# Ten shared parts between the experts instead of eight, and the slots' tokens made in two steps

## The chip, the core and the metric

The kernel runs on one core of one Trainium2 chip. The metric is the device time of one execution, in microseconds (us), as the median of several runs. The profile is one execution recorded by the hardware profiler; its span is the time from the first to the last instruction that the profiler saw. The engines go by the profile's short names: PE is TensorE (PEld its weight loads), DVE is VectorE, ACT is ScalarE, POOL is GpSimd, and SP is the engine that issues most DMAs. [...]

## The reference

One transformer block on x of shape (4, 512, 512), all in float32:

```
x = x + cross_attention(layernorm(x), context)          # 16 heads of 32; 257 image and 1344 text keys
x = x + moe(layernorm(x))                               # 2048 tokens, width D = 512

moe(h):
    scores = sigmoid(h @ router_w.T)                    # E = 32 experts, in 8 groups of 4
    keep the 3 groups whose two best (scores + bias) sum highest, then the 4 best experts in them
    w = chosen scores / their sum * 2.5
    for each expert e, the first C = 80 of its tokens (in order of token number) fill its slots
    Y[e] = (silu(Xp[e] @ W_gate[e]) * (Xp[e] @ W_up[e])) @ W_down[e]     # inner width I = 256
    out[token] += w * Y[e]                              # scattered back by token
    shared = (silu(h @ shared_gate.T) * (h @ shared_up.T)) @ shared_down.T     # inner width 512
    return out + shared
```

The shared expert sees every token; a routed expert sees only the 80 rows gathered for it.

## The kernel before

**Attention.** The four batches are worked on one after another: queries, keys and values, scores, exponentials, weighted values. The output projection, the second layernorm and the router's logits of batch b (`residual`) are interleaved with the attention of batch b + 1. For the last batch they have no attention to hide in and go into the stage described next. The normalised tokens are written to `xw_d` in device memory (one row for each token, with its 32 routing weights behind it) and, transposed, to `xnT_d`.

**The shared expert as parts.** `shared()` cuts the shared expert into parts of equal size: each is 8 matmul instructions in the profile. For every batch n of 512 tokens there are four `gate` parts (ending in a SiLU on ScalarE, L944), four `up` parts (ending in a product on VectorE, L949, which reads the gate) and four `down` parts. The downs of batches 0 and 1 end in an addition on VectorE (L967) to a tile fetched by SP (L955), which SP then stores (L968). Those of batches 2 and 3 end in a copy on ScalarE and an accumulating DMA (L972). The function gives three lists: 32 parts that run before the experts, 8 (gates and ups of batch 3) to go between the experts, and 8 (downs of batches 2 and 3) for the end. In the first list, parts 0 to 7 are gates and ups of batch 0; 8 to 19 are those of batch 1 with the downs of batch 0 among them; 20 to 31 are those of batch 2 with the downs of batch 1 among them, in the order gate, up, down, down, gate, up, down, down, gate, up, gate, up. `fetch_x` (L932) loads the next batch's transposed tokens, 1 MB, when the third gate of a batch is issued; the third gate of batch 2 is part 28.

**The stage before the experts.** A loop over the first list (index i) issues a part and then what is hung on it. The `residual` steps of the last batch hang on parts 8 to 15: fetch of the input tile (L449 adds a bias on GpSimd), projection and addition (L455), normalisation (L220), transpose (L468) and logits (L476). Every fourth part issues the three weight loads of one expert (L908), up to expert 5. `deal(i)` hands out the routing.

**The routing.** `routing(b, space)` is a list of 73 small items for 512 tokens: a sigmoid on ScalarE, then some 50 short VectorE operations that choose groups and experts (the last choice is the third L585), the store of the routing weights (L597, issued by SP), an iota on GpSimd (L610), `ranks` (four transposes on TensorE, L606, of the chosen experts, and an operation that forms a sort key, L607), and a search of 19 items that finds the 80 lowest token numbers of each expert: ten times the 8 largest (L619), and nine times these struck out (L621). Batches 0 and 1 are routed during the attention. Batch 2's list, `first`, starts behind part 2; batch 3's, `second`, at part 16, when the last logits are there. `deal(i)` hands out items in order until an amount `spent` reaches `(i - 1) * SHARE`; an item adds 0.8 when fewer than 20 are left in its list, otherwise 0.3. Items are issued behind part i on each engine, and `spent` runs on from the first list to the second.

**The tokens.** `tokens()` is called ahead of part 30. On VectorE it turns the 32 x 80 table `best` into token numbers `past` (L917 and L918), transposes it on TensorE (L920), and casts the result to integers, `tok` (L921). Behind it six indirect gathers (L993) are issued on GpSimd's queue, one for each of experts 0 to 5.

**The expert loop.** For expert e: gate and up (64 instructions, `gate_up`, L225 with SiLU at L1017 and product at L1018), weight loads for expert e + 6, the transposes of expert e + 2's tokens (`turn`, L1004, copied by L1006), the down projection of expert e - 1 (L1023), its scaling on ScalarE (L1027), its indirect scatter that adds to the output (L1028, on GpSimd's queue), and the gather for expert e + 5 behind it (L993). The parts of the second list are spread by `done * (E - 4) < n_between * e`. The third list follows the loop.

Of the kernel before, what the change touches and what calls it, by code (L numbers as in the profile page):

```python
# [58 lines left out]
@with_exitstack  # L59
def xattn_moe_kernel(ctx: ExitStack, tc: tile.TileContext, a: dict, out: bass.AP):  # L60
    nc = tc.nc

    dram = ctx.enter_context(tc.tile_pool(name="dram", bufs=1, space=DRAM))
    x1_d = dram.tile([T, D], F32, name="x1_d")

    xw_d = dram.tile([T, D + E], F32, name="xw_d")
    xnT_d = dram.tile([P, NC, T], F32, name="xnT_d")
    den_d = dram.tile([B * NC, 2 * NG4, L], F32, name="den_d")
    rec_d = dram.tile([B * NC, 2 * NG4, L], F32, name="rec_d")

    const = ctx.enter_context(tc.tile_pool(name="const", bufs=1))
    ident = const.tile([P, P], F32, name="ident")
    make_identity(nc, ident)
    mhalf = const.tile([P, 8], F32, name="mhalf")
    nc.gpsimd.memset(mhalf, -0.5)
    logits = const.tile([P, NT, E], F32, name="logits")

    with tc.manual_schedule():
        body(tc, a, ident, mhalf, logits, x1_d, xw_d, xnT_d, den_d, rec_d, out)
# [30 lines left out]
def body(ctx, tc, a, ident, mhalf, logits, x1_d, xw_d, xnT_d, den_d, rec_d, out):  # L110
# [14 lines left out]
    def psum(dt=F32):  # L125

        shape = [P, 512] if dt is F32 else [P, NQ, P]
        banks.append(banks.pop(0))
        return ring.tile(shape, dt, name="ps", tag=f"bank{banks[-1]}")
# [8 lines left out]
    def wide(name, keep=False):  # L138

        n = wides.pop(0)  # L140
        t = pt.tile([P, NC, 512], F32, name=name, tag=f"wide{n}")
        if keep:
            return t, n
        wides.append(n)
        return t

    def rowt(name):
        return row.tile([P, D], F32, name=name, tag="row")

    def held(name):  # L150
        return hold.tile([P, D], F32, name=name, tag="hold")
# [9 lines left out]
    def weight(name, tile_=None, tag=None):  # L161
        t = w.tile([P, NC, D], F32, name=name, tag=tag or name) if tile_ is None else tile_
        nc.sync.dma_start(t, a[name])
        return t
# [57 lines left out]
    def project(ps, lhsT, rhs):  # L222

        for c in range(NC):
            nc.tensor.matmul(ps, lhsT=lhsT(c), rhs=rhs(c), start=c == 0, stop=c == NC - 1)  # L225
# [678 lines left out]
    def expert_weights(e, *names):  # L904

        for name in names or ("W_gate", "W_up", "W_down"):
            t = wgp.tile([P, NI, D] if name == "W_down" else [P, NC, I], F32, name=name, tag=name)
            nc.sync.dma_start(t, a[name][e])  # L908
            weights.setdefault(e, []).append(t)

    SHARE = 2.4
    AHEAD, WEIGHTS = 6, 6

    def tokens():

        past = ew.tile([E, CAP], F32, name="past", bufs=1)
        nc.vector.tensor_scalar(past, best, T + 0.5, float(T), ALU.is_gt, ALU.mult)  # L917
        nc.vector.scalar_tensor_tensor(past, past, float(T), best, ALU.add, ALU.subtract)  # L918
        ps = psum()
        nc.tensor.transpose(ps[:CAP, :E], past, ident[:E, :E])  # L920
        nc.vector.tensor_copy(tok, ps[:CAP, :E])  # L921

    def shared():


        units = [[], [], []]
        downs = []
        xTs = {0: first_xT[0]}

        def fetch_x(n):  # L930
            xTs[n] = wide("xT")
            nc.sync.dma_start(xTs[n], xnT_d[:, :, n * L:(n + 1) * L])  # L932

        for n in range(B):
            t = {}

            def gate(ic, n=n, t=t):
                if ic == 0:
                    t["hT"] = wide("hT")
                if ic == 2 and n + 1 < B:  # L940
                    fetch_x(n + 1)
                ps = psum()
                project(ps, lambda k: sg[:, k, ic * P:(ic + 1) * P], lambda k: xTs[n][:, k, :])
                nc.scalar.activation(t["hT"][:, ic, :], ps, AF.Silu)  # L944

            def up(ic, n=n, t=t):
                ps = psum()
                project(ps, lambda k: su[:, k, ic * P:(ic + 1) * P], lambda k: xTs[n][:, k, :])
                nc.vector.tensor_tensor(t["hT"][:, ic, :], t["hT"][:, ic, :], ps, ALU.mult)  # L949
                if n == 0 and ic == NC - 1:  # L950
                    wides.append(first_xT[1])

            def fetch(j, n=n, t=t):
                t[j] = held("x1r")
                nc.sync.dma_start(t[j], x1_d[n * L + j * P:n * L + (j + 1) * P, :])  # L955

            def down(j, n=n, t=t, fetch=fetch):
                rows = slice(n * L + j * P, n * L + (j + 1) * P)
                if n < BEFORE:
                    if j == 0:  # L960
                        fetch(0)
                    if j + 1 < NQ:
                        fetch(j + 1)
                ps = psum()
                project(ps, lambda k: t["hT"][:, k, j * P:(j + 1) * P], lambda k: sd[:, k, :])
                if n < BEFORE:
                    nc.vector.tensor_tensor(t[j], t[j], ps, ALU.add)  # L967
                    nc.sync.dma_start(out[rows, :], t[j])  # L968
                    return
                y = rowt("ys")  # L970
                nc.scalar.copy(y, ps)
                nc.gpsimd.dma_start(out[rows, :], y, accum_op=ALU.add)  # L972

            to = units[n == B - 1]
            if n == B - 1:
                units[0] += downs
                downs = []
            for ic in range(NC):
                to += [partial(gate, ic), partial(up, ic)]
                if ic < 2:  # L980
                    to += downs[2 * ic:2 * ic + 2]
            downs = [partial(down, j) for j in range(NQ)]
            if n >= BEFORE:
                units[2] += downs
                downs = []
        return units
# [51 lines left out]
        return weights, gather, turn, gate_up, down  # L1038

    units, between, ends = shared()  # L1040
    wo = weight("o_w", wide("wo"))
    for u in units[:2]:
        u()
# [19 lines left out]
    def deal(i):  # L1063

        nonlocal spent
        while spent < (i - 1) * SHARE and (first or second):
            todo = first or second
            spent += 0.8 if len(todo) < 2 * CAP // 8 else 0.3
            todo.pop(0)()

    for i, u in enumerate(units):
        if i < 2:
            continue
        if i == len(units) - 2:
            for f in first + second:
                f()
            first, second = [], []
            tokens()
            for e in range(AHEAD):
                gather(e)  # L1080
        if i == ready:

            space = mid.tile([P, 2, L], F32, name="rb")
            second = sum(routing(B - 1, space.rearrange("p k t -> p (k t)")), [])
            deal(i)
        u()
        for f in side.get(i, ()):
            f()
        later.step()
        deal(i)  # L1090
        if i % 4 == 0 and i // 4 - 1 < WEIGHTS:
            expert_weights(i // 4 - 1)
# [57 lines left out]
```

## Time and profile before

| | us |
|---|---|
| median of three runs | 1709.5 |
| lowest and highest | 1707.76, 1710.98 |
| the profiled execution, its own time | 1712.07 |
| its span | 1710.4 |
| last matmul groups of the attention, about | 1338 |
| parts 2 to 31 of the shared expert, with the last residual and two routings | 1340 to 1464 |
| expert loop | 1466 to 1674 |
| downs of batches 2 and 3, and the last stores | 1674 to 1710 |

The first four rows are measured times and the profile's span; the others are read off the timeline of TensorE. In lines of the timeline the first two numbers are the start and the length in us, then engine, line, operation, the tile written and read, and in brackets how long the engine was idle before it and who released it. In the list of waits the numbers are the total, the number of waits and the longest. In the table of stages each pair is an engine's busy time with its instruction count, in the order PE, PEld, DVE, ACT, POOL, then the granted clock of TensorE (1.00 is full), the mean busy share of the 16 DMA engines and GB/s.

### The profile page before, as it was taken

How to read it: one execution, taken by the hardware profiler on the slowest of the kernel's cores; microseconds unless marked ns; L12 is line 12 of the kernel's file. 1: busy time of each engine (PE TensorE's matmuls, PEld its weight loads, DVE VectorE, ACT ScalarE, POOL GpSimd, SP SyncE). 2: the span in 40 equal slices, each digit the busy share in tenths (PEclk: the TensorE clock that was granted, in tenths of full speed). 3: DMA queues.
4: the chain of work that ended last, by engine and by line, in shares of the span. 5: the costliest groups of instructions: out<-in, count | busy, mean ns of one | idle time of the engine just before them, and what ended most of it. 6: DMA issues, size and time to landing. Idle time of an engine off the chain costs nothing. (4 is left out here: it accounts for less than half of the span.)

```text
span 1710.4 us, 29446 instructions
## 1 busy us (share of the span) xinstructions
PE 1682.0 (98%) x11753; PEld 881.9 (52%) x11753; DVE 980.2 (57%) x2012; ACT 653.4 (38%) x1382; POOL 870.3 (51%) x622
## 2 busy tenths in 40 slices
PE   8999999999999999999999999999999999999997
PEld 4564444446544444565444445654443454677673
DVE  4765554857555557876666579766656777111110
ACT  2135456611454565114555651145557310111111
POOL 3246977333669753336688533376884110333332
PEclk9999999999999999999999999999999999999999
DMA  7000000312000004020001040200002365699864
GB/s 232 1 1 1 27 27 2 114 65 71 29 2 26 26 3 164 15 81 20 2 26 27 14 153 21 83 36 10 5 15 89 114 217 188 209 285 287 268 168 61
DMA packets 67817, 136.30 MB, mean 80 GB/s; under 512 B 16096, under 2 KB 28512, under 8 KB 65632
## 3 DMA queue, kind: packets, MB, share of 16 engines
q1 hardware_dynamic: 60400, 119.91, 20.9%
q0 software_dynamic: 6272, 12.92, 4.1%
q8 instruction: 93, 1.52, 0.4%
q10 hardware_dynamic: 1008, 1.59, 0.3%
q14 instruction: 44, 0.36, 0.1%
HBM read 111.58 MB, written 22.81 MB: 79 GB/s over the span
## 5 line engine op out<-in xcount | busy, mean ns | idle before, releaser
L372 ACT ACTIVATE pT<-ps 128x512 f32<-128x512 f32 (+1 forms) x832 | 429.7, 603 | 342.2 <-PE ps L371 334.1
L334 DVE TENSOR_REDUCE mx<-ps 128x1 f32<-128x512 f32 (+1 forms) x576 | 330.9, 616 | 265.0 <-PE ps L320 265.0
L387 POOL TENSOR_TENSOR acc<-acc,pT 128x1024 f32<-128x1024 f32 x192 | 445.6, 2357 | 3.0 <-ACT pT L372 2.6
L379 PE MATMUL po<-pT,v 128*32 128x512 f32 (+2 forms) x1792 | 222.0, 603 | 0.0
L290 PEld LDWEIGHTS ps<-v_w,cT 128*128 128x128 f32 (+1 forms) x1408 | 168.9, 186 | 102.2 <-DVE mx L334 56.1
L371 PE MATMUL ps<-qT,kT 32*128 32x512 f32 (+1 forms) x1664 | 213.7, 587 | 0.0
L320 PE MATMUL ps<-kT,qT 32*128 32x512 f32 (+1 forms) x1536 | 206.2, 549 | 0.0
L290 PE MATMUL ps<-v_w,cT 128*128 128x128 f32 (+1 forms) x1408 | 197.7, 284 | 0.0
L231 PE MATMUL ps<-cT,wk 128*128 128x512 f32 (+1 forms) x384 | 156.8, 554 | 5.9 <-DMA wk<-in_k_w 5.9
L308 DVE TENSOR_REDUCE mx<-ps 128x1 f32<-128x512 f32 (+2 forms) x256 | 128.0, 561 | 5.8 <-PE ps L305 5.8
L1028 POOL DMA_INDIRECT out<-y,tok x32 | 45.5, 1420 | 136.8 <-DMA out<-y,tok 68.4
L231 PEld LDWEIGHTS ps<-cT,wk 128*128 128x128 f32 x384 | 71.1, 194 | 75.9 <-issue 55.7
L368 PEld LDWEIGHTS <-pick 32*128 32x128 bf16 (+1 forms) x832 | 21.6, 91 | 165.8 <-issue 164.0
L298 ACT COPY v<-ps 128x128 f32<-128x128 f32 (+1 forms) x208 | 59.7, 287 | 117.7 <-PE ps L290 117.3
L238 POOL TENSOR_TENSOR sq_k<-sq_k,sq 128x512 f32<-128x512 f32 (+2 forms) x48 | 49.6, 1033 | 103.3 <-ACT sq L235 103.0
L1018 DVE TENSOR_TENSOR ehT<-ehT,ps 128x160 f32<-128x160 f32 x32 | 10.3, 321 | 159.7 <-ACT ehT L1017 159.7
L394 POOL TENSOR_TENSOR acc<-pT 128x1024 f32<-128x1024 f32 x24 | 56.1, 2359 | 86.9 <-ACT pT L372 54.3
L387 POOL TENSOR_TENSOR pT<-pT 65x1024 f32<-65x1024 f32 x24 | 56.0, 2354 | 86.7 <-PE po L379 77.9
L387 DVE TENSOR_TENSOR acc<-acc,pT 128x1024 f32<-128x1024 f32 (+1 forms) x72 | 97.7, 1404 | 2.1 <-ACT pT L372 2.1
L320 PEld LDWEIGHTS ps<-kT,qT 32*128 32x128 f32 x1536 | 82.0, 183 | 30.8 <-issue 10.1
L379 PEld LDWEIGHTS po<-pT,v 128*32 128x32 f32 (+2 forms) x1792 | 34.7, 107 | 118.6 <-issue 109.3
L368 PE MATMUL ps<-mT,pick 32*128 32x512 bf16 (+1 forms) x832 | 82.5, 385 | 2.5 <-ACT mT L359 2.5
(209 smaller groups left out, 2194.4 us busy)
## 6 DMA issues: line engine op xcount, KB each, us to landing
W_gate<-in_W_gate SPq DMA_DIRECT2D x32, 512.0 KB, 4.9
W_up<-in_W_up SPq DMA_DIRECT2D x32, 512.0 KB, 5.2
W_down<-in_W_down SPq DMA_DIRECT2D x32, 512.0 KB, 5.7
rb<-rec_d SPq DMA_DIRECT2D x64, 128.0 KB, 2.7
xt<-in_x SPq DMA_DIRECT2D x30, 256.0 KB, 2.7
cT<-in_ctxT SPq DMA_DIRECT2D x7, 1024.0 KB, 9.3
wki<-in_k_img_w SPq DMA_DIRECT2D x4, 1024.0 KB, 10.4
wo<-in_o_w SPq DMA_DIRECT2D x4, 1024.0 KB, 5.0
```

The costliest lines, as they stand in the source:

```text
L231: nc.tensor.matmul(ps[:, :n], lhsT=wt[:, k, c * P:(c + 1) * P], rhs=xT[:, k, to], start=k == 0, stop=k == NC - 1)
L290: nc.tensor.matmul(ps[lo:hi, :], lhsT=cTs[bl][:, k, at:at + hi - lo], rhs=ws[bl == NB - 1][:, k, c * P:(c + 1) * P], start=k == 0, stop=k ...
L298: nc.scalar.copy(v[:n, t, :], ps[:n])
L308: nc.vector.tensor_reduce(mx[:, qt, g, bl:bl + 1], ps[:, :n], AX.X, ALU.max, negate=True)
L320: nc.tensor.matmul(ps[:, j * n:(j + 1) * n], lhsT=qT[r:r + HD, c, q * P:(q + 1) * P], rhs=kT[r:r + HD, c, k0:k0 + n], start=True, stop=True,)
L334: nc.vector.tensor_reduce(mx[:, qt, g, i:i + 1], ps[:, :m], AX.X, ALU.max, negate=True)
L368: nc.tensor.matmul(ps[:n], lhsT=pick[r:r + HD, kind(t), :n], rhs=mT[r:r + HD, :], start=True, stop=False)
L371: nc.tensor.matmul(ps[:n], lhsT=kT[r:r + HD, c, t * P:t * P + n], rhs=qT[r:r + HD, c, :], start=False, stop=True)
L372: nc.scalar.activation(pT[:n, g, :], ps[:n], AF.Exp)
L379: nc.tensor.matmul(po[r:r + HD, :], lhsT=v[rows, t, r:r + HD], rhs=pT[rows, g, :], start=start, stop=stop)
L387: (nc.vector if idle else nc.gpsimd).tensor_tensor(to[rows, h, :], to[rows, h, :], pT[rows, h, :], ALU.add)
L394: (nc.vector if idle else nc.gpsimd).tensor_tensor(acc[:, h, :], pTs[0][:, h, :], pTs[1][:, h, :], ALU.add)
```

## The change

Two parts, the last gate and the last up of batch 2, go from the end of the first list to the front of the second. The first list is then 30 parts long and ten parts are spread between the experts. `tokens` is split. Its two VectorE operations, now `kept_tokens`, are issued ahead of part 27 (they were ahead of part 30), and what is left of `tokens`, with the six gathers, ahead of part 28, which again is two parts before the list ends. What is left of the routing by then is issued ahead of part 27. `SHARE`, by which `deal` hands out the routing, rises from 2.4 to 2.7.

```diff
-    SHARE = 2.4
+    SHARE = 2.7
     AHEAD, WEIGHTS = 6, 6
 
-    def tokens():
+    def kept_tokens():
 
         past = ew.tile([E, CAP], F32, name="past", bufs=1)
         nc.vector.tensor_scalar(past, best, T + 0.5, float(T), ALU.is_gt, ALU.mult)
         nc.vector.scalar_tensor_tensor(past, past, float(T), best, ALU.add, ALU.subtract)
+        return past
+
+    def tokens(past):
+
         ps = psum()
         nc.tensor.transpose(ps[:CAP, :E], past, ident[:E, :E])
         nc.vector.tensor_copy(tok, ps[:CAP, :E])
...
     units, between, ends = shared()
+    units, between = units[:-2], units[-2:] + between
     wo = weight("o_w", wide("wo"))
...
     for i, u in enumerate(units):
         if i < 2:
             continue
-        if i == len(units) - 2:
+        if i == len(units) - 3:
             for f in first + second:
                 f()
             first, second = [], []
-            tokens()
+            past = kept_tokens()
+        if i == len(units) - 2:
+            tokens(past)
             for e in range(AHEAD):
                 gather(e)
```

## The prediction

> **What bounds the kernel now.** I read the page first, then the table of stages, the waits of TensorE alone, and the chain and the timelines around each of those waits.
>
> ```profile
> PE 1682.0 (98%) x11753; PEld 881.9 (52%) x11753; DVE 980.2 (57%) x2012; ACT 653.4 (38%) x1382; POOL 870.3 (51%) x622
> 1440.00:1480.00 40.00, 38.09 (x158) 21.65 (x156) 14.47 (x30) 3.08 (x6) 8.21 (x8) 1.00 0.53 166
> 1560.00:1600.00 40.00, 39.45 (x251) 29.23 (x249) 4.70 (x12) 6.29 (x13) 12.59 (x11) 1.00 0.92 285
> 1600.00:1640.00 40.00, 37.19 (x227) 26.65 (x228) 4.61 (x13) 6.46 (x13) 14.41 (x13) 1.00 0.94 281
> ```
>
> TensorE (first pair of numbers of a stage row, then weight loads, VectorE, ScalarE, GpSimd, clock, DMA share, GB/s) has work almost all the time. No matmul is added or dropped, so only its idle time can change. From the last attention to the end it idles in three stages: 1.9 us in 1440 to 1480, 0.55 in 1560 to 1600, 2.8 in 1600 to 1640. Its waits from 1330 us on name them:
>
> ```profile
> PE ps L1004 <- DMA xp<-xw_d,tok: 2.3, 1, 2.3
> PE ps L920 <- DVE past L918: 1.2, 1, 1.2
> PE ps L1004 <- ACT ehT L1017: 0.9, 2, 0.5
> PE ps L225 <- DVE xpT L1006: 0.7, 1, 0.7
> ```
>
> **The loop's stall.** The chain shows where the first of them comes from:
>
> ```profile
> 1584.46 7.10 DMA out<-y,tok
> 1592.38 5.94 DMA out<-y,tok
> 1599.14 6.34 DMA out<-y,tok
> 1608.03 6.11 DMA xp<-xw_d,tok
> 1614.27 0.47 PE ps L1004 x4
> ```
>
> Each expert's scatter (L1028) waits for the landing of the one before, and the gather of expert e+6 (L993) is issued behind the scatter of e on the same queue. From the scatter of expert 4 (1505.64 us) to that of expert 18 (1606.30) there are 14 periods in 100.66 us: 7.19 each. TensorE needs 5.53 us for an expert (1478.88 to 1484.41) and 3.43 for a shared part. With eight parts over 28 turns that is 5.53 + 8/28 x 3.43 = 6.51: quicker than the chain of DMAs, so its lead of gathers is used up. The timeline has the turns (L1004) at 1565.19, 1600.37, 1606.20 and 1614.27 later than the matmuls ahead of them allow by 0.61, 0.64, 0.28 and 2.50 us: **4.03 us**. The first two are booked to ScalarE, but gathers 17 and 22 were issued at 1558.45 and 1594.11, 6.7 and 6.3 us earlier, about a landing (6.11 in the chain). I read all four as gathers.
>
> **What moving two parts into the loop does.** Two matmul groups of 8 (2 x 3.43 us) leave from before the loop. The count in the source puts the ten parts after experts 1, 3, 6, 9, 12, 15, 17, 20, 23, 26, where eight stood after 1, 4, 8, 11, 15, 18, 22, 25. At the turns made beside experts 15 and 20, TensorE has done one part more than before (3.43 us), beside 21 and 22 two more (6.86). Up to there the missed time added up to 0.61, 1.25, 1.53 and 4.03. The cover suffices at each, by 2.83 us at the last. The chain itself starts alike: two parts lie ahead of the output of expert 4 before and after. I take **-4.0 us**; kept between 0 and -4.0.
>
> **Tokens a part sooner.** Before, L917 and L918 stand on VectorE behind the product of the last gate and up, which waits for TensorE:
>
> ```profile
> 1456.33 0.69 DVE L949 TENSOR_TENSOR hT<-hT,ps 128x512 f32<-128x512 f32 x1 [3.91 <-PE ps L225]
> 1457.15 0.23 DVE L918 SCALAR_TENSOR_TENSOR past<-past,best 32x80 f32<-32x80 f32 x1
> 1457.43 0.22 PE L920 MATMUL ps<-ident,past 32*80 32x32 f32 x1 [1.21 <-DVE past L918]
> ```
>
> The first matmuls of parts 29 and 31 are at 1452.62 and 1461.12: two parts should take 6.87, they took 8.50. Of the 1.63, some 0.13 is the transpose and **1.5** the wait. Afterwards the two small operations (0.18 + 0.23) follow the residual add of part 26, one whole part (3.43) ahead of the transpose, so the wait goes: -1.5. This needs the search to be done by then. Its last maximum is now dealt after part 24, not 27; following VectorE's durations it ends near 1442.3 on the old clock, and part 26 ends at 1445.8. If that cover were lost, the 1.5 comes back. The last wait of the list (0.7, the copy of the turned tokens behind the last product) is left as it is.
>
> What is late next: the cast (L921) stands behind the residual add of part 27, so the first gather starts some 1.3 us after that part (1450.5 on the old clock), with 5.7 us to the first turn instead of 6.4. And the 1 MB load of the last batch's tokens (L932, issued at 1450.53, 5.6 us to land), which was over before the gathers, now runs beside them. No row shows that pair. Nearest are these gathers' own landings (3.2 us median on a quiet queue) and those of the whole loop (5.3 median, 7.7 largest). The second gather starts 1.5 later and is needed 0.4 later, 4.6 us after its start: late by 0 at 3.2, 0.7 at 5.3, 3.1 at 7.7. I take **+0.3**, since one load shares the engines here and three streams do in the loop.
>
> **Routing dealt denser.** `deal` spends 0.3 for each of a routing's first 54 items and 0.8 for the 19 of its search. The item `ranks` (four transposes on TensorE, L606) is the 54th, and the last choice of experts, which it reads, the 44th. Item 54 is dealt once (i-1) x SHARE exceeds 53 x 0.3 = 15.9: behind part 8 at 2.4, behind part 7 at 2.7. The choice needs 12.9: behind part 7, now 6. So TensorE meets the transposes 3.43 us sooner. Can VectorE keep up?
>
> ```profile
> 1360.73 3.60 PE L225 MATMUL ps<-xT,shared_gate 128*128 128x512 f32 x8
> 1364.16 0.60 PE L606 MATMUL ps<-ident,space 128*32 128x128 f32 x4
> 1364.02 0.46 PEld L606 LDWEIGHTS ps<-ident,space 128*32 128x32 f32 x4 [0.52 <-issue]
> 1359.84 1.29 POOL L449 TENSOR_TENSOR xt<-xt,o_b 128x512 f32<-128x512 f32 x1 [5.51 <-DMA xt<-in_x]
> 1360.04 1.24 DVE L585 TENSOR_TENSOR space<-space 128x128 f32<-128x128 f32 x1
> 1362.05 0.68 DVE L949 TENSOR_TENSOR hT<-hT,ps 128x512 f32<-128x512 f32 x1
> 1363.61 0.29 DVE L585 TENSOR_TENSOR space<-space 128x128 f32<-128x128 f32 x1
> ```
>
> It can't. From 1346.01 to 1363.90, the end of the choice, it has no gap, and it can't begin sooner, since the sigmoid ends at 1345.98. Already now the weight load follows the choice by 0.12 and the matmul by 0.26. Two things shorten VectorE's way. The product of part 7 (L949, net 0.60) now stands behind the choice. And L585 at 1360.04 took 1.24 where its sisters take 0.29, beside GpSimd's L449; that add needs a load which now stands in SP's queue behind the store of the routing weights (L597, dealt behind part 7, one part ahead of the load), so it moves to about 1368: -0.95. The choice ends at 1363.90 - 0.60 - 0.95 = 1362.35, the transposes start at 1362.61 where 1360.73 would be free: **+1.9 us**. The Trainium skill, "SBUF — State Buffer", section "SBUF: two separate sides", says the two engines' shared pair is an exclusive lock held for a whole instruction, taken by whoever comes first. By it the 0.95 goes with the collision; by the row alone, kept as VectorE's own, the wait is 2.85 and the total 0.95 worse. I take the first. The displaced add may block VectorE near 1368, where it next waits for TensorE by over 1 us: no cost.
>
> For the second routing the item numbers start from 31.4 spent: `ranks` moves from part 21 to 19, the choice from 20 to 18. The burst behind part 16 grows from 15 to 31 VectorE operations.
>
> ```profile
> 1425.59 0.29 DVE L585 TENSOR_TENSOR rb<-rb 128x128 f32<-128x128 f32 x1
> 1427.72 0.10 PEld L606 LDWEIGHTS ps<-ident,rb 128*32 128x32 f32 x1 [0.24 <-issue]
> ```
>
> From 1408.23 to the choice's end at 1425.88 VectorE waits 2.36 + 1.35 for products that it would no longer wait for, and one product (0.60) falls behind: the choice ends at 1421.55, the transposes start 0.26 later, at 1421.81, where TensorE would be at 1421.28: **+0.5 us**.
>
> The rule that speaks against these new waits is in "TensorE: Matmul & The Clock Gate", section "What's actually happening": an idle window of about 3.4 us drops the array to half its clock, for as long again. Here the wait of 2.33 us at 1614 left the granted clock at 1.00. By the row 1.9 us cost nothing more; by the rule, were the window filled, half speed over 3.4 us would add an estimated 1.7. I take the row.
>
> SP's other moves cost nothing: the weights of expert 4 (issued from 1410.65) now wait behind the second routing's store until some 1424, and are first read 60 us later; the residual tiles queued behind them are first needed by part 22, at 1432. The later residual steps keep their 3 to 6 us between a normalised tile and its transpose.
>
> **Sum.** -4.0 - 1.5 + 1.9 + 0.5 + 0.3 = **-2.8 us**. The profiled execution has a span of 1710.4 and 1.7 around it, 1712.1; it becomes 1707.6 and 1709.3. The runs' median is 2.6 below the profiled one, so the difference is put on it: 1709.5 - 2.8 = **1706.7 us**.
>
> **Rivals.** (B) *VectorE isn't late at the transposes*, because stretched operations shrink when the GpSimd work moves (L569, L570 and L579 also took 1.0 to 1.3 beside it): both waits fall to about 0.4 in all, -4.0 - 1.5 + 0.4 + 0.3 = -4.8, 1704.7. Against it: the GpSimd scaling that stretches those three doesn't move. (C) *The loop keeps its stalls*, because the chain, not TensorE, sets the pace: -4.0 shrinks to -2, or the gathers beside the load are late by 2: -0.8, 1708.7. For it: the DMA share is 0.92 to 0.94. Against: the same weights are asked for over a longer time. (D) *Slower: the scatter chain lengthens in the loop.* From scatter 4 to 18 each microsecond on the period costs 14, once the 2.83 of cover is used. To be 0.2% slower the stall must be 3.4 + 2.8 = 6.2 on top, a period of 7.19 + 9.0/14 = 7.84, that is, landings of 7.0 instead of 6.4; at 7.84 the time is 1712.9. Single landings of 7.5 are in the trace, which speaks for it; the thinner weight traffic against.
>
> **How the numbers follow.** A measurement of this kernel tells some 0.2% (3.4 us) from no change: 1706.1 and 1712.9 are the bounds. As worked out (A): 55%, own range 1705.2 to 1708.4, a third of it below 1706.1. B 18%, faster; C 11%, within; D 16%, slower. Faster 0.18 + 0.18 = 0.36, within 0.37 + 0.11 = 0.48, slower 0.16. The range reaches below B, to 1703.5, and to D's beginning, 1713.0.
>
> **What would show it.** In the profile after: no wait at L920; turns in the loop without waits for xp; a wait of about 1.9 us of TensorE's weight load at the first L606 after 1340 and one of 0.5 at the next; the last maximum over 4 us ahead of L917; the second gather landing within 0.7 us of its turn. Wrong it would be if the period of the scatters is well off 7.2, or the first L606 waits under 1 or over 3 us.

## The result, and the profile after

The changed kernel takes 1716.7 us as a median of 22 runs; the kernel before, run in turn with it, 1708.8. The ratio is 1.0032, with a 95% interval of 1.0023 to 1.0040: slower by some 0.3%, where a gain of 2.8 us was forecast. The ratio is smaller than the ratio of the medians, since the runs of the changed kernel fall into two groups with nothing in between: 8 at 1709.3 to 1711.0 us with a mean granted clock of 0.997 to 0.998, and 14 at 1715.2 to 1718.6 with 0.993 to 0.994. The means, 1714.7 and 1709.2, give the ratio.

The profile after is of one of the eight short executions (1710.2, span 1708.5; before 1712.1 and 1710.4). In the changed kernel the lines from the token function on are numbered four higher: the turn is L1008, the transpose of the tokens L924. First the waits of TensorE from 1330 us on, then the timelines of TensorE, GpSimd and VectorE at the places named in the prediction:

```profile
PE ps L1008 <- DMA xp<-xw_d,tok: 1.6, 2, 1.3
PE ps L606 <- DVE space L585: 1.4, 1, 1.4
```

```profile
1357.57 3.60 PE L225 MATMUL ps<-xT,shared_up 128*128 128x512 f32 x8
1362.58 0.61 PE L606 MATMUL ps<-ident,space 128*32 128x128 f32 x4 [1.42 <-DVE space L585]
...
1419.71 3.60 PE L225 MATMUL ps<-xT,shared_up 128*128 128x512 f32 x8
1423.44 0.61 PE L606 MATMUL ps<-ident,rb 128*32 128x128 f32 x4
...
1451.46 0.22 PE L924 MATMUL ps<-ident,past 32*80 32x32 f32 x1
1455.15 3.60 PE L225 MATMUL ps<-xT,shared_up 128*128 128x512 f32 x8
1460.08 0.49 PE L1008 MATMUL ps<-ident,xp 80*128 80x80 f32 x4 [1.34 <-DMA xp<-xw_d,tok]
1460.85 0.47 PE L1008 MATMUL ps<-ident,xp 80*128 80x80 f32 x4 [0.27 <-DMA xp<-xw_d,tok]
1461.16 2.01 PE L225 MATMUL ps<-xpT,W_gate 128*128 128x80 f32 x16
```

```profile
1360.09 0.29 DVE L585 TENSOR_TENSOR space<-space 128x128 f32<-128x128 f32 x1
1362.24 0.29 DVE L585 TENSOR_TENSOR space<-space 128x128 f32<-128x128 f32 x1
...
1443.40 0.77 DVE L619 MAX8 best<-merged 32x8 f32<-32x592 f32 x1
...
1448.73 0.18 DVE L917 TENSOR_SCALAR past<-best 32x80 f32<-32x80 f32 x1
```

```profile
1368.00 1.27 POOL L449 TENSOR_TENSOR xt<-xt,o_b 128x512 f32<-128x512 f32 x1 [12.15 <-DMA xt<-in_x]
```

A part takes 3.43 us, so the first L606 could have begun at 1361.00 and the second at 1423.14: they are 1.58 and 0.30 late. The transpose of the tokens (L924) has no wait, and the last maximum ends 4.6 us ahead of L917. The displaced addition (L449) is at 1368, and the L585 that took 1.24 beside it takes 0.29. In the loop no turn waits: from its first matmul (1461.16) to the last stage's (1671.99) it takes 210.83 us, with ten parts, where 208.11 and two parts of 3.43 make 214.97. The loop gave 4.1 in this pair of executions.

The term that came out larger than forecast is at the entry of the loop: the first turn, free at 1458.58, begins at 1460.08. It is 1.5 late, and the matmuls of expert 0 begin 2.58 behind the last part's end, where it was 1.42 before. In all, from part 2 to the loop the change loses 1.8 and in the loop it gains 4.1: -2.4. A later start of part 2 (0.28) and a longer tail (0.2) leave the -1.9 between the two spans.

None of this explains the 14 runs near 1717. For that the lowered mean clock was the only lead.

### The profile page after: what moved, and what is told of

Read it like the earlier page. It is cut to its first block, busy times and chain, and to the rows that moved or that the text cites. A ratio compares the mean times of both kernels' runs of the same rounds, so it can differ in the third digit from the quotient of the medians.

```text
span 1708.5 us, 29447 instructions
## 1 busy us (share of the span) xinstructions
PE 1682.0 (98%) x11753; PEld 881.4 (52%) x11753; DVE 977.2 (57%) x2012; ACT 653.4 (38%) x1382; POOL 869.8 (51%) x622
```

## The experiments

Two theories were put up. **G, the clock gate**: behind one of the new waits the granted clock of TensorE falls for some 14 us; at the routing (first L606) or at the entry of the loop (first two L1008). **D, memory**: the longer group has a longer scatter chain in the loop. "Long" and "short" are executions of the group near 1717 and of the one near 1710. Five runs are of unchanged kernels, for their traces; the others have edits of a line or a few.

### The changed kernel again (after_again, after_look, after_look2)

> The changed kernel once more, unchanged. Its executions fall into two groups, near 1710 us at a mean clock of 0.997 and near 1717 us at 0.993 to 0.994. Theory G (clock gate): the longer group is one in which a new wait of TensorE (1.6 us at the first L606 of the last stage, or 1.6 us in all at the first two L1008) is followed by some 14 us at half clock; a trace of a long execution shows granted clock well under 1.00 right behind one of these waits and no other new wait. Theory D (memory): the longer group has a longer scatter chain; a trace of it shows turns L1008 in the loop waiting for xp for 5 us or more in all.

> The changed kernel unchanged, for one more trace, in the hope of an execution of the longer group (some 3 in 4 are). Theory G: behind a wait of TensorE of 1 to 3 us whole groups of 8 matmuls take about twice 3.6 us, as the group behind the wait at L924 did in the kernel with dealing at 2.4 (5.40 us); together 7 us. Theory D: no such group, but turns in the loop that wait for xp.

> The changed kernel unchanged, one more trace. In the longer group G expects a granted clock near 0.5 for some 14 us behind the wait at the first turns; in the shorter group a clock of 1.00 and a wait under 2 us.

The first gave 5 runs at 1709.5 to 1710.6 and 15 at 1716.0 to 1717.8: the two groups are the kernel's, not a day's. All three traces, though, were of the shorter group (1710.0, 1709.4, 1709.5), with a wait of 1.2 to 1.4 at the first L606, of 1.3 to 2.0 in all at the entry, and the clock at 1.00 from the first L606 to the end of the loop. So there is no trace of the longer group of the changed kernel itself; those below are of kernels one edit away from it.

### The dealing back at 2.4 (share_24), the dealing alone (share_alone), the parts alone (parts_alone)

```diff
share_24, against the kernel after:
-    SHARE = 2.7
+    SHARE = 2.4
share_alone, against the kernel before:
-    SHARE = 2.4
+    SHARE = 2.7
parts_alone, against the kernel before:
     units, between, ends = shared()
+    units, between = units[:-2], units[-2:] + between
```

> Ten parts and the split tokens stay, the dealing goes back to 2.4. The wait at both L606 goes (1.6 + 0.3 us), three search items are left to the flush ahead of part 27. If the wait at the first L606 triggers the loss of clock (G at the routing), the group near 1717 is gone and the time is about 1708. If the wait at the entry of the loop triggers it (G at the entry), both groups stay, near 1708 and 1715. Theory D: the loop is the same, so both groups stay too.

> The kernel before with the denser dealing alone (2.7). The waits at the two L606 come (1.6 + 0.3 us), the parts and the tokens stay as before. G at the routing: a group of executions 7 us longer, near 1716 to 1718, beside one near 1709 to 1712. G at the entry and D: no such group, 1709 to 1712 in all, which is the time before plus 1.9 less what the later start of the loop gives back.

> The kernel before with the two parts moved and nothing else: tokens unsplit ahead of part 28, dealing at 2.4. The loop's stalls go (0 to 4.0 us), the wait at L920 stays or grows, since the last search items are dealt behind part 27, directly ahead; no wait at L606. G at the routing: one group, near 1707 to 1709. G at the entry or D: a second group 7 us longer.

| | runs | ratio to before |
|---|---|---|
| share_24 | 12 at 1709.1 to 1711.8 | 1.0008 (1.0000 to 1.0017) |
| share_alone | 7 at 1709.6 to 1710.6, 5 at 1712.0 to 1713.3 | 1.0010 (1.0001 to 1.0019) |
| parts_alone | 1 at 1709.3, 14 at 1712.1 to 1713.9 | 1.0015 (1.0007 to 1.0023) |

None has the group near 1717. The dealing alone has the wait at the first L606 (1.23 us in its trace) and no such group, so this wait by itself is not the trigger. Its trace is of one of the five slower runs (1712.9), and shows another loss: a wait in the loop is followed by 3.4 us of half clock, which cost 1.7 more (the first group below takes 3.28 instead of 1.88, the shared part behind it 3.94 instead of 3.60).

```profile
1587.92 0.47 PE L1004 MATMUL ps<-ident,xp 80*128 80x80 f32 x4 [1.41 <-DMA xp<-xw_d,tok]
1588.22 3.28 PE L1023 MATMUL ps<-W_down,ehT 128*80 128x512 f32 x4
```

The other two kernels were slower than expected: share_24 was not near 1708, nor parts_alone near 1707 to 1709. The trace of share_24 shows why. Its search ends directly ahead of the tokens, and the transpose waits 2.69 us. Here is TensorE's timeline, then the table of stages (PE, PEld, DVE, ACT, POOL, clock, DMA share, GB/s):

```profile
1451.97 0.22 PE L924 MATMUL ps<-ident,past 32*80 32x32 f32 x1 [2.69 <-DVE past L918]
1452.12 5.40 PE L225 MATMUL ps<-xT,shared_gate 128*128 128x512 f32 x8
```

```profile
1452.00:1454.00 2.00, 2.00 (x4) 0.93 (x5) 0.61 (x2) 0.00 (x0) 1.08 (x1) 0.59 0.31 110
1454.00:1456.00 2.00, 2.00 (x4) 0.80 (x3) 0.00 (x0) 0.00 (x0) 1.40 (x3) 0.56 0.84 221
1456.00:1458.00 2.00, 2.00 (x6) 0.95 (x5) 0.00 (x0) 0.45 (x1) 1.48 (x2) 1.00 0.98 317
```

The group of 8 behind the wait takes 5.40 instead of 3.60: the clock falls to a half for 3.4 us, which costs another 1.8. In parts_alone the wait is 3.60 and the group behind it takes 6.73:

```profile
1453.06 0.27 PE L920 MATMUL ps<-ident,past 32*80 32x32 f32 x1 [3.60 <-DVE past L918]
1453.25 6.73 PE L225 MATMUL ps<-xT,shared_gate 128*128 128x512 f32 x8
```

So a wait under 3 us can take the clock with it, which the prediction had ruled out. Both kernels also lack the wait for gathers at the entry. In share_24 the first gather still starts beside the 1 MB load:

```profile
1452.92 1.22 POOL L997 DMA_INDIRECT xp<-xw_d,tok  x1 [46.89 <-DVE tok L925]
1452.97 0.58 SPq L936 DMA_DIRECT2D xT<-xnT_d  x1
```

But the slowed group puts the first turn off to 1460.79, 7.9 us after the gather's start, where the changed kernel has 5.9 (1452.65 to 1458.58). So share_24 removed both waits at once and can't tell the two places apart; share_alone speaks against the routing, which left the entry to be tested.

### The load a gate later, the first routing at 2.4, and both (fetch_late, first_24, both)

```diff
fetch_late, against the kernel after:
-                if ic == 2 and n + 1 < B:
+                if ic == (3 if n == 2 else 2) and n + 1 < B:
first_24, against the kernel after:
-        while spent < (i - 1) * SHARE and (first or second):
+        while spent < (i - 1) * (SHARE if i >= ready else 2.4) and (first or second):
both: the two together
```

> The changed kernel with the 1 MB load for the last batch issued one gate later (behind expert 1, at the fourth gate of batch 2), so that it doesn't run beside the first gathers. The wait of 1.6 to 2.0 us at the first two turns L1008 shrinks to under 0.5; the waits at L606 stay. G at the entry: the group near 1717 is gone, the time is near 1708.3. G at the routing, and D: the group stays, near 1715.

> The changed kernel with the first list dealt at 2.4 and the second at 2.7. The wait of 1.2 to 1.6 us at the first L606 goes, that at the entry of the loop stays. G at the routing: the group near 1717 is gone, the time is near 1708.4. G at the entry, and D: both groups stay, each 1.4 us lower, near 1708.5 and 1715.5.

> Both edits together: load for the last batch one gate later, first list dealt at 2.4. No wait over 0.7 us is left between 1340 us and the end of the loop. G, at either place: one group, near 1706.5 to 1707, below the kernel before (1707 to 1711). D: the longer group stays 7 us above the shorter.

| | runs | ratio to before |
|---|---|---|
| fetch_late | 12 at 1707.7 to 1709.2 | 0.9991 (0.9982 to 1.0000) |
| first_24 | 8 at 1707.7 to 1708.7, 4 at 1716.5 to 1717.9 | 1.0007 (0.9990 to 1.0024) |
| both | 13 at 1705.9 to 1707.3, 1 at 1708.9 | 0.9982 (0.9974 to 0.9990) |

This tells the places apart. With the load moved out of the gathers' way, the entry keeps only the copy's wait, and the longer group is gone; the wait at the first L606 is still there:

```profile
PE ps L606 <- DVE space L585: 1.4, 1, 1.4
PE ps L225 <- DVE xpT L1010: 0.7, 1, 0.7
```

With the first L606 mended instead and the entry left, the group stays:

```profile
PE ps L1008 <- DMA xp<-xw_d,tok: 2.2, 2, 1.8
```

With both, the kernel is faster than before by 0.18%, with an interval of 0.10 to 0.26%.

### The load twice, and the tokens a part later (load_twice, late_tokens)

```diff
load_twice, against the kernel after:
             nc.sync.dma_start(xTs[n], xnT_d[:, :, n * L:(n + 1) * L])
+            if n == B - 1:
+                nc.sync.dma_start(xTs[n], xnT_d[:, :, n * L:(n + 1) * L])
late_tokens, against the kernel after:
-        if i == len(units) - 2:
+        if i == len(units) - 1:
             tokens(past)
```

> The changed kernel with the 1 MB load for the last batch issued twice in a row into the same tile, so that the first gathers meet twice the traffic. G at the entry: the wait at the first two turns L1008 grows from 1.1 to 1.8 us to 2.5 us or more, and with it the long group takes in nearly all executions; the trace then shows a granted clock near 0.5 behind that wait, for about 14 us if this is what the 7 us are, and the time is 1717 or more. If the wait costs only itself, the time rises by 1 to 3 us, to 1711 to 1713, in one group.

> The changed kernel with the transpose of the tokens and the six gathers issued one part later, ahead of the last part before the loop, with the load for the last batch then ahead of them. The first turn has one part (3.43 us) less to wait behind: a wait of 2.3 to 4 us at L1008, with little of it from the load. G at the entry: the clock falls behind it in all executions, and the time is the wait plus some 7 us above the 1708.5 of the kernel without the wait, near 1718. If only the meeting with the load does the harm: 1711 to 1712.5, clock at 1.00.

Neither made the wait longer, so neither tests its length. In load_twice the second load was issued only at 1457.62, 6.4 us behind the first, and the first gathers, started from 1451.12 on, did not meet twice the traffic. In late_tokens the gathers start 2.9 us behind the load (1454.41 and 1451.48) and land in 3.0. The runs: load_twice 5 at 1709.9 to 1710.7 and 15 at 1716.0 to 1718.1, as the changed kernel; late_tokens 9 at 1707.8 to 1709.6 and 3 at 1714.6 to 1715.0. But both traces were of long executions. load_twice, at 1716.7 with a clock of 0.993, timeline of TensorE and table of stages (the second load shifts the lines: here L1010 is the turn, L1029 the down projection):

```profile
1453.61 3.60 PE L225 MATMUL ps<-xT,shared_up 128*128 128x512 f32 x8
1458.43 0.50 PE L1010 MATMUL ps<-ident,xp 80*128 80x80 f32 x4 [1.22 <-DMA xp<-xw_d,tok]
1459.24 0.47 PE L1010 MATMUL ps<-ident,xp 80*128 80x80 f32 x4 [0.32 <-issue]
1459.55 2.99 PE L225 MATMUL ps<-xpT,W_gate 128*128 128x80 f32 x16
1462.33 3.62 PE L225 MATMUL ps<-xpT,W_up 128*128 128x80 f32 x16
...
1473.64 3.62 PE L1029 MATMUL ps<-W_down,ehT 128*80 128x512 f32 x4
1477.05 3.74 PE L225 MATMUL ps<-xT,shared_gate 128*128 128x512 f32 x8
1480.63 1.91 PE L225 MATMUL ps<-xpT,W_gate 128*128 128x80 f32 x16
```

```profile
1458.00:1460.00 2.00, 1.25 (x12) 1.13 (x13) 0.74 (x3) 0.00 (x0) 0.42 (x1) 1.00 1.03 234
1460.00:1462.00 2.00, 2.00 (x13) 2.00 (x13) 0.24 (x1) 0.00 (x0) 0.00 (x0) 0.57 1.05 303
1462.00:1464.00 2.00, 2.00 (x11) 2.00 (x11) 0.00 (x0) 0.00 (x0) 0.00 (x0) 0.50 1.07 299
...
1474.00:1476.00 2.00, 2.00 (x3) 0.51 (x2) 0.41 (x2) 0.00 (x0) 0.00 (x0) 0.50 0.75 242
1476.00:1478.00 2.00, 2.00 (x4) 0.86 (x3) 0.00 (x0) 0.68 (x1) 0.00 (x0) 0.66 0.05 21
1478.00:1480.00 2.00, 2.00 (x6) 0.95 (x5) 0.00 (x0) 0.00 (x0) 1.50 (x1) 1.00 0.79 254
```

This is the 7 us. The first turn is 1.4 late (1458.43 against 1453.61 + 3.43), no more than in the short executions. Then the clock falls to a half and stays there for 17 us, through both first experts. From expert 0's first matmul to the shared part behind expert 1 it takes 17.50 us (1459.55 to 1477.05), where the profile of the changed kernel has 9.48 (1461.16 to 1470.64): 8.0 us more. (The two spans are 6.5 apart, since this execution reaches part 2 at 1338.87, 1.4 sooner.) The matmuls of 80 columns take 3.62 for a group instead of 1.95, with TensorE's weight loads busy without a gap. From 1500 us on the clock is 1.00 and no turn waits: theory D falls. The trace of late_tokens shows the same, 15.96 us for this stretch with a clock of 0.50 from 1462 to 1474. There the change of one part has shifted the waits (0.26 and 0.90, clock gone by 1461), so not even 1.4 in one piece is needed.

Slices of 0.1 us give the lengths of the losses. The clock is at a half for 3.41 us in share_24 and in share_alone, for 6.83 in parts_alone, 13.65 in late_tokens (1460.88 to 1474.53) and 17.07 in load_twice (1460.27 to 1477.34): one, two, four and five times 3.41. So the clock here fell and rose in whole steps of 3.41 us, and each step costs about half its length, 1.7 us.

### The first wide part sooner (dense_first), and the kernel before again

```diff
-        while done < n_between and done * (E - 4) < n_between * e:
+        while done < n_between and done * (E - 4) <= n_between * e:
```

> The changed kernel with the first of the ten parts behind expert 0 instead of expert 1 (and one later part behind 14 instead of 15); the wait at the first turns stays. In the two traces with the lost clock it comes back in the first stretch of matmuls of 512 columns, behind expert 1, after some 16 us. If the narrow matmuls of the experts (80 columns) keep it down, the clock now comes back behind expert 0, after some 10 us, and the longer group lies 2 to 4 us lower, at 1713 to 1715, with the shorter one unchanged near 1710. If the length of the loss is a fixed time, the longer group stays at 1716 to 1718.

Four runs are at 1709.6 to 1710.2, eleven at 1711.9 to 1715.1, one at 1717.6; the ratio to before is 1.0027 (1.0018 to 1.0035). The longer group came down by about 3 us, as expected if the clock returns at the first wide part (a shared part, with matmuls of 512 columns). It also spread, and its trace was of a short execution, so the losses themselves are not seen.

> The kernel before, unchanged, for a second trace of it: its profile on record was of an execution at 1712.1, 3 us above the median, and had 4.0 us of stalls in the loop. If the stalls are there in every execution, a trace of one near 1708 shows them too, and something else is shorter; if they come and go, the turns L1004 of such an execution wait for xp by under 1 us.

> As the run ahead of it: a third trace of the kernel before. Stalls of the loop near 0 in an execution near 1708 us, 3 to 4 us in one near 1712.

These two were at 1710.2 and 1708.9 us. The list of waits of TensorE, the first two lines of before_again, the last of before_third:

```profile
PE ps L1004 <- DMA xp<-xw_d,tok: 1.2, 1, 1.2
...
PE ps L1004 <- ACT ehT L1017: 0.4, 1, 0.4
```

```profile
PE ps L1004 <- DMA xp<-xw_d,tok: 0.8, 1, 0.8
```

The stall of the loop comes and goes: 3.2 us of booked waits in the profile on record, 1.6 in the second trace, 0.8 in the third, with spans of 1710.4, 1708.5 and 1707.2. The loop's own time, from its first matmul to the last stage's, says the same: 208.11, 206.06 and 204.97 us. Against the changed kernel's 210.83, less two parts, the gain is 4.1, 2.1 or 1.0. The execution on record was one with a large stall, near 3 us above the median.

## Why the prediction was wrong

- **The rule of the clock gate, "I take the row"**: this step failed. The row was one wait of 2.33 us in the loop that left the clock at 1.00. From it the prediction put the loss of clock at nothing for every new wait, and weighed it at the routing only. The same trace held a row that says the opposite, earlier, in the attention, where TensorE waits for the keys. Here it is with a row of the table of stages behind it (clock 0.52), then the same place in before_again, where the clock stays at 1.00:

```profile
707.20 1.14 PE L305 MATMUL ps<-kT,qT 32*128 32x512 f32 x8 [2.06 <-DVE kT L259]
708.94 3.79 PE L231 MATMUL ps<-cT,wk 128*128 128x320 f32 x8
710.00:712.00 2.00, 2.00 (x5) 1.35 (x4) 2.00 (x4) 0.00 (x0) 0.00 (x0) 0.52 0.00 0
```

```profile
708.86 1.14 PE L305 MATMUL ps<-kT,qT 32*128 32x512 f32 x8 [2.05 <-DVE kT L259]
710.38 2.32 PE L231 MATMUL ps<-cT,wk 128*128 128x320 f32 x8
```

This wait, 2.0 to 2.3 us long in all sixteen traces, took the clock for 3.41 us in four of them (before, after, after_again, dense_first) and left it in twelve. So a wait of this size takes the clock in some executions and not in others, and one row can't rule it out. The estimated 1.7 was right for one step (1.7 here, from 707.20 to the end of the second group against the same in before_again; 1.7 in share_alone, 1.8 in share_24). At the loop's entry, behind a wait of 1.4, the runs show four or five steps, 6.5 to 8.0 us, and a longer group in two thirds to three quarters of the executions of the changed kernel. The Trainium skill, "TensorE: Matmul & The Clock Gate", section "What's actually happening", says that the window of 3.4 us in which activity is counted runs free and doesn't start with the work. The steps of 3.41 us agree with that, and so does a wait which takes the clock in one execution and leaves it in the next. Its condition of one idle window does not hold here as a bound: in the 3.41 us ahead of the fall TensorE was busy for 1.9 us in load_twice, 2.3 in late_tokens and 1.4 at L305, by the modelled ends of its matmuls. Only share_24 (0.7) and parts_alone (0.3) come near to it.
- **"+0.3" for the gathers beside the load**: right in mechanism and mis-sized. The prediction asked only when the second gather lands; the first was the later one, since its turn begins 7.4 us after its start (1452.65 to 1460.08) where 5.9 were free. The first turn is 1.5 late and the second another 0.3 to 0.4; against the 0.7 wait for the copy, which they swallow, the entry costs 1.2. The range given there, 0 to 3.1, held it. What was missed is what follows at this place: eight transposes of 80 columns, then two experts of narrow matmuls, under which the clock didn't come back in the traces of load_twice and late_tokens; the times of dense_first agree.
- **"-4.0" for the loop**: held for the pair of profiles (4.1), and the mechanism was right, since with ten parts no turn waits in any trace but those at the entry. As a gain on the median it was mis-sized: against two other executions of the kernel before it was 2.1 and 1.0. The difference was taken from an execution 2.6 above the median and put on the median.
- **"-1.5" for the tokens**: right, no wait at L924; the search ended 4.6 us ahead.
- **"+1.9" and "+0.5" at the two L606**: 1.58 and 0.30. The sequence was as worked out, down to the displaced addition and its 0.95: the first choice ends at 1362.53, where 1362.35 plus the later start of the stage makes 1362.63. A TensorE that is already waiting follows it by 0.05 and not by 0.26, which is most of the difference in both.
- **The rivals**: D, the one on the slow side, was the wrong mechanism: the period of the scatters from expert 4 to 18 is 6.97 us, shorter than the 7.19 before. B did not occur; of C the late gathers came, with 1.2 of its 2. Neither of the two signs that were to show the prediction wrong came: the period is near 7.2, and the first L606 waits 1.4. No rival had the clock as its deciding step.

The short runs lie 1.3 above the kernel before (1710.1 in their middle, against 1708.8). Against the third trace of the kernel before, of an execution at 1708.9, the change loses 1.8 up to the loop and gains 1.0 in it, +0.8; half a microsecond stays open. That the new waits make up the stage's loss shows on one chip: from part 2 to the loop it is 120.65 us in the trace of after_look and 118.12 in that of `both`, 2.5 less.

Open: what decides between the groups in a single execution, and why their shares differ so much from kernel to kernel. The two long executions that were traced reach part 2 at 1338.87 and 1339.19 us, the fourteen other traces at 1339.71 to 1340.31, so the moment at which the program meets the steps of the clock may decide; two traces don't show it. The wait at the first L606 may matter by the moment to which it shifts the entry (about 7 in 10 long with it, 4 in 12 without), but the changed kernel and first_24 were timed on different chips, and this wasn't tried on one. No trace shows that the changed kernel's own long runs lose the clock at the entry; load_twice, which has the same two groups at the same clocks, and the disappearance of the group in fetch_late stand for it.

## What to carry to other kernels

Price a new wait of TensorE by what comes behind it. Where a wait took the clock, it cost itself and 1.7 to 3.1 us more ahead of wide matmuls, and 6.5 to 8.0 more ahead of a row of narrow ones. One wait that left the clock alone doesn't show that the next will: look at the clock behind every wait of the trace, and in a second trace. A load that only the future needs can be moved out of the way of one that TensorE is about to wait for; here that one line was worth the whole loss. And before a stall in one profile is counted as a gain, look at a second execution: 4.1 us here were 2.1 and 1.0 against two others.

## What the runs showed of the hardware that was not expected

A granted clock at 0.50 while TensorE was never idle: for 12 us in load_twice (1460 to 1472) its matmuls had 80 columns and its weight loads were busy 2.00 of every 2.00 us, and the clock came back only with matmuls of 512 columns, 3.7 us after the first of them in load_twice (1473.64 to 1477.34) and 1.6 in late_tokens. The nine stretches of half clock that were measured, six of them 3.41 us and the others 6.83, 13.65 and 17.07, are all whole multiples of 3.41 us. And a kernel on a single core can have two groups of executions 7 us apart, told by the mean clock, 0.997 and 0.993.
